# A decoder layer: the score scale moved into the keys, and one output projection by seven products

## The chip, the cores and the metric

The kernel runs on one core of a Trainium2 chip. The metric is the device time of one execution in microseconds; of several runs the median counts. A core has TensorE (PE in the profile), VectorE (DVE), ScalarE (ACT), GpSimd (POOL) and SyncE (SP, which here only issues DMAs). Each engine works its own queue in order, and they wait for each other by semaphores.

## The reference

One layer of a decoder in fp32, with two batch elements of 512 positions and 512 features, layer norm after each residual sum:

```python
x = layernorm(x + attn(x))          # 16 heads of 128, weights = codes * scales (blocks of 32 rows)
x = layernorm(x + xattn(x, memory)) # one head over 1024 memory rows, only the 54 largest scores kept
x = layernorm(x + ffn(x))           # silu(gate) * up, 2048 hidden

# attn
q, k, v = x @ wq + bq, x @ wk + bk, x @ wv + bv
attn = softmax(q @ k.T / sqrt(128)) @ v        # per head
out  = attn @ wo + bo
# xattn
scores = coef * (x @ W_q.T) @ memory.T
att    = softmax(where(scores < 54th largest, -inf, scores))
out    = (att @ memory) @ W_o.T
```

## The kernel before, in words

**Products of blocks.** Nearly all large products are done in blocks of two by two with seven half-size products instead of eight. `seven` issues them: the stationary side and the moving side are each split into four blocks, and sums of blocks are prepared ahead (`combine_a`, `combine_b`, `sums_a`, `sums_b`; four block sums each). Products 1, 6 and 7 accumulate in turn in one PSUM bank `r`, and after each of them ScalarE copies the running sum to `u` (`keep`, line 197, with a bias). So `r` can take the next product only after the copy. Products 2, 5, 4 and 3 go to two or three areas `z`; VectorE adds `z` and `u` in two steps, `on_second` after product 4 and `on_first` after product 3. Product 3 is held back until the next group has begun (`open_product`, `close`). With `late`, product 2 is issued ahead of product 1.

**PSUM.** `r` has two banks, `t` two (single-bank tiles), and `z` two double tiles of two banks. Scores use `z` too: `sc` for the query tiles 0 and 1 takes one, for 2 and 3 the other.

**Attention.** A unit is one head of one element, 32 in all; four units with the same element make a phase, which has one product for the values (`values`) and one for the output (`project`). For each unit `queries_keys` makes q and k (`rqk`, `zqk` in the profile, k added on line 711, q on 712). `weights` makes scores (`sc`, line 748), their negative maximum on VectorE (line 759), multiplies it by 1/sqrt(128) on ScalarE (line 760), takes the exponential with scale 1/sqrt(128) and that bias (line 763, with the row sum), multiplies by the inverse sum (line 772), transposes 32 by 32 blocks on VectorE (line 775) and finishes the transposition with 16 DMAs (line 783). `attend` multiplies with the values two units later (`av`, line 795).

**Second half.** For element 0 the cross-attention runs among the last units of element 1; its search for the 54th largest score (lines 485 to 503) is spread over VectorE's queue. For element 1 the cross queries and scores follow (`seven_xquery`, `seven_xscores`, tiles `xq`, `xs`), and the search and transposition are spread over the feed-forward of element 0: `up` works one 128-wide hidden block after another (`wgu` loaded by SP, block sums `wc` by POOL, `rgu` and `zgu` on TensorE, SiLU on line 1087, gate product on line 1088, `hc` sums of the hidden activations), and `down` multiplies eight hidden blocks back (`rpd`, `zpd`). After `up(0, 1)` and before `down(0, 1)` stands `xattend(1)`: the attention output `xo` by two groups of seven products (`rxav`, `zxav`), then the output product `xpo` (line 597) by plain full-width matmuls, four for each of four position tiles. Layer norm "b" of element 1, its transposition `x2T` and the feed-forward of element 1 follow.

**Order.** The program is written as above, and the framework's scheduler then orders the instructions of each engine; it may place a product of one group between those of another. Semaphores are counted for each engine. Tiles of one tag share a place in memory: a new tile waits until the readers of the old one are done.

```python
    hc = up(0, 1, nc.vector, search1, combine_wdn(0, 1))
    for _ in search1:
        pass
    for _ in xattend(1, ("ot0", "ot1")):
        pass
    layernorm(1, "b")
```

Of the kernel before, what the change touches and what calls it, by code (L numbers as in the profile page):

```python
# [10 lines left out]
F32 = mybir.dt.float32  # L11
AF = mybir.ActivationFunctionType
ALU = mybir.AluOpType
# [11 lines left out]
def decoder_layer(  # L25
# [52 lines left out]
    def place(tag, shape, name):  # L78
        return sb.tile([P, *shape], F32, tag=tag, name=name)
# [85 lines left out]
    def close():  # L165

        if open_product:
            open_product.pop()()

    def seven(name, stat, mov, cols, on_second, on_first, bias=(0.0, 0.0), late=False, piece=None):  # L170


        n = seven_count[0] % 2
        seven_count[0] += 1
        r = bank("r", f"r{name}")[:, :HS]
        if piece:

            zs = [bank("t", f"z{name}_{i}")[:, :HS] for i in range(2)] + [double(f"z{name}", (4, HS))[:, 2, :]]
        else:
            z = double(f"z{name}", (4, HS))  # L180
            zs = [z[:, i, :] for i in range(3)]
        u = place(f"u{n}", (3, HS), f"u{name}")

        def product(i, o, start=True):
            left, right = chunks(stat[i]), chunks(mov[i])
            for k in range(len(left)):
                nc.tensor.matmul(  # L187
                    o,
                    left[k][:, cols],
                    right[k],  # L190
                    start=start and k == 0,
                    stop=k == len(left) - 1,
                    skip_group_check=not start,
                )

        def keep(i, at):
            nc.scalar.activation(u[:, i, :], r, AF.Identity, bias=at)  # L197

        if late:
            product(2, zs[1])  # L200
        product(1, r)
        keep(0, bias[0])
        if not late:
            product(2, zs[1])
        product(5, zs[2])
        product(6, r, False)
        keep(1, bias[0])
        close()
        product(7, r, False)
        keep(2, bias[1])  # L210
        if piece:
            piece(zs[2], u[:, 2, :], 1, 1)
            piece(zs[1], u[:, 0, :], 0, 0)
        product(4, zs[0])
        if piece:
            piece(zs[0], u[:, 2, :], 1, 0)
        else:
            on_second(z[:, 0::2, :], u[:, 2:3, :].to_broadcast([P, 2, HS]))

        def rest():  # L220
            product(3, zs[2], False)
            if piece:
                piece(zs[2], u[:, 1, :], 0, 1)
            else:
                on_first(z[:, 1:3, :], u[:, 0:2, :])

        open_product.append(rest)
# [348 lines left out]
    def xattend(b, ot_tags):  # L576

        oth = [place(tag, (2, S), f"xo{b}_{n}") for n, tag in enumerate(ot_tags)]
        ot = [t[:, n, :] for t in oth for n in range(2)]
        for m in range(HK):  # L580
            seven(
                f"xav{b}_{m}",
                mems[b],
                ats[b],
                slice(m * P, (m + 1) * P),
                lambda z, u, m=m: put(ot[HK + m], z, u, b == 1),
                lambda z, u, m=m: put(ot[m], z, u, b == 1),
            )
            yield
        close()  # L590

        order = [(t, k) for t in range(NT) for k in (0, 2, 3, 1)]
        if b == 0:
            order = [(0, 0), (0, 2), (0, 3), (1, 0), (1, 2), (1, 3), (0, 1), (1, 1)] + order[8:]
        po = [bank("rt"[t % 2], f"xpo{b}_{t}") for t in range(NT)]
        for t, k in order:
            nc.tensor.matmul(
                po[t],
                ot[k][:, t * P : (t + 1) * P],
                xw["wo"][:, k, :],  # L600
                start=(k == 0),
                stop=(k == 1),
                skip_group_check=True,
            )
            if k == 1:
                nc.vector.tensor_add(res[b, t], po[t], res[b, t])
# [93 lines left out]
    def queries_keys(u):  # L700

        g, b, j = units[u]
        h = g * GH + j
        qt = place(f"q{u % 2}", (2, HS), f"q{u}")
        kt = place(f"k{u % 2}", (2, HS), f"k{u}")
        seven(
            f"qk{u}",
            qkw[u],
            xcs[b],
            slice(0, P),  # L710
            lambda z, c: nc.vector.tensor_add(kt, z, c),
            lambda z, c: nc.vector.tensor_add(qt, z, c),
            (bq_sb[:, h : h + 1], bk_sb[:, h : h + 1]),
        )
        qs[u], ks[u] = qt.rearrange("p n s -> p (n s)"), kt.rearrange("p n s -> p (n s)")

    def first_queries_keys():

        z = double("zqk0", (2, S))
        for k in range(KD):  # L720
            for n in range(2):
                nc.tensor.matmul(
                    z[:, n, :],
                    raw["qk0"][0][:, k, n, :],
                    xts[0][:, k, :],
                    start=k == 0,
                    stop=k == KD - 1,
                )
        qs[0] = place("q0", (S,), "q0")
        ks[0] = place("k0", (S,), "k0")  # L730
        nc.scalar.activation(qs[0], z[:, 0, :], AF.Identity, bias=bq_sb[:, 0:1])
        nc.scalar.activation(ks[0], z[:, 1, :], AF.Identity, bias=bk_sb[:, 0:1])

    def weights(u):

# [2 lines left out]
        for t in range(NT):  # L738
            if t % 2 == 0:

                if u == 0 and t:
                    pair = [bank("t", f"sc{u}_{t}_{n}") for n in range(2)]
                else:
                    scs = double(f"sc{u}_{t}")
                    pair = [scs[:, n, :] for n in range(2)]
                nms = small.tile([P, 2], F32, tag="nm", name=f"nm{u}_{t}")
                for n in range(2):
                    nc.tensor.matmul(  # L748
                        pair[n],
                        q[:, (t + n) * P : (t + n + 1) * P],  # L750
                        k,
                        start=True,
                        stop=True,
                    )
                if u == 0 and t:
                    for n in range(2):
                        nc.vector.reduce_max(nms[:, n : n + 1], pair[n], axis=AX.X, negate=True)
                else:
                    nc.vector.reduce_max(nms, scs, axis=AX.X, negate=True)  # L759
                nc.scalar.mul(nms, nms, HSCALE)  # L760
            pr = place(f"p{t}", (S,), f"p{u}_{t}")
            sm = small.tile([P, 1], F32, tag="sm", name=f"sm{u}_{t}")
            nc.scalar.activation(  # L763
                pr,
                pair[t % 2],
                AF.Exp,
                bias=nms[:, t % 2 : t % 2 + 1],
                scale=HSCALE,
                accum_out=sm,
            )  # L770
            nc.vector.reciprocal(sm, sm)  # L771
            nc.scalar.activation(pr, pr, AF.Copy, scale=sm)  # L772


            nc.vector.transpose(  # L775
                tq[:, :, :, t, :].rearrange("p n k c -> p k n c"),
                pr.rearrange("p (k n a) -> p k n a", n=NB, a=BLK),
            )
# [81 lines left out]
    for k in range(KD):  # L860
        nc.scalar.dma_start(out=first[0][k], in_=wqk_first[0][:, k])
        nc.sync.dma_start(out=xts[0][:, k, :], in_=xT[0, k * P : (k + 1) * P, :])
    nc.sync.dma_start(out=bqkv_sb, in_=bqkv)
    for n in range(2):
        nc.scalar.dma_start(out=first[1][n], in_=wqk_first[1][:, n * HK : (n + 1) * HK])
    for h in range(2):
# [171 lines left out]
            nc.gpsimd.tensor_tensor(c[3][:, w], b10[:, w], c[1][:, w], ALU.subtract)  # L1038
            yield

    def up(b, half, eng, search=iter(()), between=iter(())):


        hs, c = [], []
# [20 lines left out]
        for n in range(NH):  # L1065
# [7 lines left out]
            )  # L1073
            if n > 1:
                next(between, None)
            ut = place(f"k{n % 2}", (2, HS), f"ut{i}_{b}")

            def second(z, u, ut=ut):
# [25 lines left out]
    def down(b, half, hc, last_one=False):  # L1104

        for s in range(NT // 2):

            def add(z, u, t):
                o = res[b, t].rearrange("p (c f) -> p c f", c=2)
                if last_one:  # L1110
                    nc.vector.tensor_add(o, o, u)
                    nc.vector.tensor_add(o, z, o)
                else:
                    nc.vector.tensor_add(o, z, o)  # L1114
                    nc.gpsimd.tensor_tensor(o, o, u, ALU.add)  # L1115
# [51 lines left out]
    down(0, 0, hc)  # L1167
    load_wdn(0, 1)
    search1 = chain(search1, turn_weights(1, 2, ("ot0", "ot1"), ("cmb0", "cmb1"), ("v0", "work")))
    hc = up(0, 1, nc.vector, search1, combine_wdn(0, 1))  # L1170
    for _ in search1:
        pass
    for _ in xattend(1, ("ot0", "ot1")):
        pass
    layernorm(1, "b")
    turn_x(1, "v0", "v1", "x2T")
    combine_turned(nc.vector, 1, "v0", "x2")
# [79 lines left out]
```

## Time and profile before

| | |
|---|---|
| median of 3 runs | 1094.98 us (1094.96 to 1095.44) |
| the profiled execution | 1093.37 us |
| its span, first to last instruction | 1091.6 us |
| mean granted TensorE clock | 0.999 |
| PE busy | 1076.9 us (99%) |
| DVE, ACT, POOL busy | 628.3, 411.4, 546.5 us |
| cross-attention output of both elements (`xpo`, line 597) | 64 passes, 28.3 us busy |
| maximum's scaling (line 760) | 64, 12.9 us busy |

A matmul in fp32 is two instructions in the trace, here called passes, each with its weight load (PEld). The mean length of a pass in the profile (381 ns at 256 columns, 592 at 512) is longer than the distance between two of them, since they overlap; the distance is what counts. A number in brackets after a row is the engine's idle time just before it, with what ended it. A line number can be that of a helper: all products of `seven` stand under line 187, all copies of `keep` under 197, and the tile names tell them apart.

### The profile page before, as it was taken

Reading aid. Unit: us, or ns where it says so; the run is one execution under the profiler, and the core shown is the slowest. Engines: PE = TensorE matmul, PEld = TensorE weight load, DVE = VectorE, ACT = ScalarE, POOL = GpSimd, SP = SyncE. Lnnn points to the kernel's source line nnn. Section 1 sums busy time; section 2 is a strip of 40 time slices with the busy share of each in tenths; the row PEclk is TensorE's granted clock in tenths of the full one; section 3 lists DMA queues with packets and bytes.
Section 4 is the critical chain, followed back from the end, with each engine's and each line's share of the span. In section 5 each row is a group of like instructions: output and inputs, shape, how many; then the busy total and the mean of one; then the engine's idle time right before and its main releaser. Section 6 shows DMA issues by size and latency. Waiting matters only on the chain.

```text
span 1091.6 us, 12812 instructions
## 1 busy us (share of the span) xinstructions
PE 1076.9 (99%) x4230; PEld 794.4 (73%) x4230; DVE 628.3 (58%) x1027; ACT 411.4 (38%) x937; POOL 546.5 (50%) x546
## 2 busy tenths in 40 slices
PE   9999999999999999999999999999999999999997
PEld 6676776677677677665666568668888886888886
DVE  5445445346345446643898874568999634543354
ACT  3454435335344433733444453322543211221221
POOL 4965715845844844513852553651565720454620
PEclk9999999999999999999999999999999999999999
DMA  9635546555554365535332535431223411522201
GB/s 349 193 101 156 189 107 209 183 162 153 182 173 125 122 195 146 185 90 178 135 116 80 158 98 205 135 97 39 97 77 119 132 40 25 169 82 73 97 20 39
DMA packets 66256, 142.70 MB, mean 131 GB/s; under 512 B 12560, under 2 KB 12560, under 8 KB 66192
## 3 DMA queue, kind: packets, MB, share of 16 engines
q1 hardware_dynamic: 65328, 139.80, 40.6%
q10 hardware_dynamic: 864, 2.10, 0.5%
q8 instruction: 34, 0.56, 0.2%
q14 instruction: 30, 0.25, 0.1%
HBM read 99.90 MB, written 2.10 MB: 93 GB/s over the span
## 4 chain that ended last, share of the span: by engine, by line
PE 75%; DVE 13%; ACT 4%; DMA 3%; SPq 2%; issue 1%; POOL 1%; ACTq 0%; DVEq 0%; POOLq 0%
PE sc L748 9%; PE av L795 9%; PE zqk L187 8%; PE zgu L187 7%; PE rqk L187 6%; PE zo L187 5%; PE rgu L187 5%; PE zv L187 5%; PE ro L187 4%; PE zpd L187 3%; PE rv L187 3%; DVE work L491 3%; DVE top L494 3%; PE zxav L187 2%; PE rpd L187 2%; PE rxav L187 2%
## 5 line engine op out<-in xcount | busy, mean ns | idle before, releaser
L795 PE MATMUL av<-pt,v 128*128 128x512 f32 x256 | 121.8, 592 | 0.0
L748 PE MATMUL sc<-k,q 128*128 128x512 f32 x256 | 116.8, 597 | 0.0
L759 DVE TENSOR_REDUCE nm<-sc 128x2 f32<-128x1024 f32 x63 | 76.8, 1223 | 66.8 <-PE sc L748 66.8
L107 POOL TENSOR_TENSOR wc<-wqk 128x256 f32<-128x256 f32 x31 | 24.2, 782 | 162.6 <-PE zqk L187 161.6
L775 DVE STREAM_TRANSPOSE tq<-p 128x512 f32<-128x512 f32 x128 | 85.0, 699 | 35.1 <-ACT p L772 28.7
L748 PEld LDWEIGHTS sc<-k,q 128*128 128x128 f32 x256 | 47.6, 190 | 58.0 <-issue 50.9
L648 POOL TENSOR_TENSOR wqk<-wqk,sqk 128x512 f32<-128x512 f32 x52 | 65.0, 1269 | 46.9 <-DMA wqk<-in_wqk 33.6
L763 ACT ACTIVATE p<-sc,nm 128x512 f32<-128x512 f32 x128 | 86.8, 685 | 1.5
L772 ACT ACTIVATE p<-p,sm 128x512 f32<-128x512 f32 x128 | 86.2, 722 | 0.6 <-DVE sm L771 0.6
L197 ACT ACTIVATE ugu<-rgu 128x256 f32<-128x256 f32 x96 | 36.0, 378 | 99.2 <-PE rgu L187 97.1
L795 PEld LDWEIGHTS av<-pt,v 128*128 128x128 f32 x256 | 48.6, 190 | 30.5 <-issue 26.8
L197 ACT ACTIVATE uqk<-rqk,bqkv_sb 128x256 f32<-128x256 f32 x93 | 43.9, 472 | 64.4 <-PE rqk L187 64.4
L187 PE MATMUL rgu<-x2c,wc 128*128 128x256 f32 x256 | 66.1, 381 | 1.0 <-ACT ugu L197 1.0
L187 PE MATMUL rqk<-x0c,wc 128*128 128x256 f32 x248 | 64.8, 384 | 0.3
L187 PEld LDWEIGHTS rqk<-x0c,wc 128*128 128x128 f32 x248 | 45.5, 190 | 19.4 <-ACT uqk L197 9.9
L107 POOL TENSOR_TENSOR wc<-wgu 128x256 f32<-128x256 f32 x32 | 25.4, 794 | 67.9 <-DMA wgu<-in_wgu 35.1
L494 DVE MAX8 top<-work 128x8 f32<-128x1024 f32 x48 | 58.7, 1223 | 0.9
L1115 POOL TENSOR_TENSOR res<-res,upd 128x512 f32<-128x512 f32 x12 | 15.8, 1313 | 78.3 <-DVE res L1114 73.7
L187 PEld LDWEIGHTS rgu<-x2c,wc 128*128 128x128 f32 x256 | 48.2, 190 | 8.8 <-ACT ugu L197 1.7
L813 ACT ACTIVATE ot<-av,bqkv_sb 128x512 f32<-128x512 f32 x28 | 19.2, 686 | 81.1 <-PE av L795 81.1
L491 DVE MATCH_REPLACE8 work<-top,work 128x1024 f32<-128x1024 f32 x40 | 48.4, 1210 | 0.0
L648 POOL TENSOR_TENSOR wv<-wv,sv 128x512 f32<-128x512 f32 x24 | 29.9, 1269 | 31.1 <-DMA wv<-in_wv 31.1
(285 smaller groups left out, 2432.0 us busy)
## 6 DMA issues: line engine op xcount, KB each, us to landing
pt<-tq SPq DMA_DIRECT2D x512, 64.0 KB, 2.0
wgu<-in_wgu SPq DMA_DIRECT2D x32, 512.0 KB, 3.2
wqk<-in_wqk SPq DMA_DIRECT2D x26, 512.0 KB, 3.9
sqk<-in_wqk_s SPq DMA_DIRECT2D x26, 512.0 KB, 4.0
wdn<-in_wdn SPq DMA_DIRECT2D x8, 1024.0 KB, 5.8
sv<-in_wv_s SPq DMA_DIRECT2D x14, 512.0 KB, 5.7
wv<-in_wv SPq DMA_DIRECT2D x7, 1024.0 KB, 5.6
wo<-in_wo SPq DMA_DIRECT2D x7, 1024.0 KB, 5.6
```

The lines of the kernel that those rows point to most:

```text
L107: eng.tensor_tensor(c[0], a10, a11, ALU.add)
L187: nc.tensor.matmul(o, left[k][:, cols], right[k], start=start and k == 0, stop=k == len(left) - 1, skip_group_check=not start,)
L197: nc.scalar.activation(u[:, i, :], r, AF.Identity, bias=at)
L491: nc.vector.match_replace(work, top, src, LOWEST)
L494: nc.vector.max(top, work)
L648: eng.tensor_tensor(part[:, w], codes[:, w], sct[:, w], ALU.mult)
L748: nc.tensor.matmul(pair[n], q[:, (t + n) * P : (t + n + 1) * P], k, start=True, stop=True,)
L759: nc.vector.reduce_max(nms, scs, axis=AX.X, negate=True)
L763: nc.scalar.activation(pr, pair[t % 2], AF.Exp, bias=nms[:, t % 2 : t % 2 + 1], scale=HSCALE, accum_out=sm,)
L772: nc.scalar.activation(pr, pr, AF.Copy, scale=sm)
L775: nc.vector.transpose(tq[:, :, :, t, :].rearrange("p n k c -> p k n c"), pr.rearrange("p (k n a) -> p k n a", n=NB, a=BLK),)
L795: nc.tensor.matmul(av, vs[u // GH][:, k, j * P : (j + 1) * P], pt[:, :, k, :], start=(k == 0), stop=(k == NT - 1),)
```

## The change

**Scale.** The factor 1/sqrt(128) goes into the keys. `seven` gets a `scale` for its third copy, k is made with `scalar_tensor_tensor` (z times the factor plus u), the key's bias is scaled once into `bks`, and the scaling of the maximum and the scale of the exponential go.

**Output of the second element by seven products.** For element 1 `xattend` makes block sums of `xo` as its chunks come (VectorE, `first`), and multiplies with the output weights by two groups `xpo` of `seven`. The weights' sums `woc` are made by POOL in the place "v1". This whole cross-attention is moved ahead of the last hidden block of `up(0, 1)` (`other`); `up`'s search is emptied first.

**With it.** `late` issues product 4 early too, right behind product 2 (cross scores of element 1 and the new product). `down` of the second half (`if half`) adds `u` and `z` both on VectorE, where before POOL added `u` (element 0).

```diff
     def seven(..., late=False, piece=None, scale=1.0):
...
         if late:
             product(2, zs[1])
+            product(4, zs[0])
         product(1, r)
...
-        keep(2, bias[1])
+        keep(2, bias[1], scale)
...
-        product(4, zs[0])
+        if not late:
+            product(4, zs[0])
...
+        o4, sums = [t[:, :, h] for h in (slice(0, HS), slice(HS, S)) for t in oth], []
+        if b == 1:
+            c12 = [place(f"p{n}", (HK, HS), f"xoc{n}") for n in range(2)]
+            c4 = place("wqk0", (HK, HS), "xoc_4")
+
+        def first(z, u, m):
+            put(ot[m], z, u, b == 1)
+            if b == 1:
+                c = [f[:, m : m + 1] for f in (*c12, c4)]
+                sums.append(sums_a(nc.vector, o4, [[f] for f in c], [slice(m, m + 1)]))
+                next(sums[-1])
+                for left in sums if m else ():
+                    next(left)
...
         close()
+        if b == 1:
+            stat = ALEFT(o4, (*c12, o4[2], c4))
+            for s in range(NT // 2):
+
+                def add(z, u, t):
+                    o = res[b, t].rearrange("p (c f) -> p c f", c=2)
+                    nc.vector.tensor_add(o, o, u)
+                    nc.vector.tensor_add(o, z, o)
+
+                seven(
+                    f"xpo{b}_{s}",
+                    stat,
+                    xw["woc"],
+                    slice(s * P, (s + 1) * P),
+                    lambda z, u, s=s: add(z, u, 2 + s),
+                    lambda z, u, s=s: add(z, u, s),
+                    late=s == 0,
+                )
+            close()
+            return
...
-            lambda z, c: nc.vector.tensor_add(kt, z, c),
+            lambda z, c: nc.vector.scalar_tensor_tensor(kt, z, HSCALE, c, ALU.mult, ALU.add),
             lambda z, c: nc.vector.tensor_add(qt, z, c),
-            (bq_sb[:, h : h + 1], bk_sb[:, h : h + 1]),
+            (bq_sb[:, h : h + 1], bks[:, h : h + 1]),
+            scale=HSCALE,
...
-                nc.scalar.mul(nms, nms, HSCALE)
...
                 bias=nms[:, t % 2 : t % 2 + 1],
-                scale=HSCALE,
...
+    bks = const.tile([P, H], F32, name="bks")
+    nc.scalar.mul(bks, bk_sb, HSCALE)
...
+            if other and n == NH - 1:
+                for _ in search:
+                    pass
+                for _ in other:
+                    if sums:
+                        sums.pop()()
...
-                if last_one:
+                if half:
                     nc.vector.tensor_add(o, o, u)
                     nc.vector.tensor_add(o, z, o)
...
-    hc = up(0, 1, nc.vector, search1, combine_wdn(0, 1))
-    for _ in search1:
-        pass
-    for _ in xattend(1, ("ot0", "ot1")):
-        pass
+    def attended_early():
+        xw["woc"] = combine_b(nc.gpsimd, blocks(xw["wo"]), place("v1", (4, HK, HD), "woc"))
+        yield from xattend(1, ("ot0", "ot1"))
+
+    hc = up(0, 1, nc.vector, search1, combine_wdn(0, 1), attended_early())
```

The changed order that the scheduler makes of it is known too, without times: ScalarE takes three of a unit's four exponentials before the multiplications by the inverse sums and the fourth after three of these; TensorE's next `rqk` begins after the scores instead of before them; and the products of the last hidden block stand behind those of the new output product.

More of the change, by code (lines that the diff above doesn't have):

```diff
@@ L168, in close, with seven @@
             open_product.pop()()
-    def seven(name, stat, mov, cols, on_second, on_first, bias=(0.0, 0.0), late=False, piece=None):
+    def seven(name, stat, mov, cols, on_second, on_first, bias=(0.0, 0.0), late=False, piece=None, scale=1.0):
         n = seven_count[0] % 2
@@ L194, in product, with keep @@
                 )
-        def keep(i, at):
-            nc.scalar.activation(u[:, i, :], r, AF.Identity, bias=at)
+        def keep(i, at, scale=1.0):
+            nc.scalar.activation(u[:, i, :], r, AF.Identity, bias=at, scale=scale)
         if late:
             product(2, zs[1])
+            product(4, zs[0])
         product(1, r)
@@ L586, in xattend @@
                 lambda z, u, m=m: put(ot[HK + m], z, u, b == 1),
-                lambda z, u, m=m: put(ot[m], z, u, b == 1),
+                lambda z, u, m=m: first(z, u, m),
             )
@@ L731, in first_queries_keys @@
         nc.scalar.activation(qs[0], z[:, 0, :], AF.Identity, bias=bq_sb[:, 0:1])
-        nc.scalar.activation(ks[0], z[:, 1, :], AF.Identity, bias=bk_sb[:, 0:1])
+        nc.scalar.activation(ks[0], z[:, 1, :], AF.Identity, bias=bks[:, 0:1], scale=HSCALE)
     def weights(u):
@@ L1039, in combine_wdn, with up @@
             yield
-    def up(b, half, eng, search=iter(()), between=iter(())):
+    def up(b, half, eng, search=iter(()), between=iter(()), other=None):
         hs, c = [], []
```

## The prediction

> **What bounds the kernel now.** I read the page first, then the groups kept apart by form, then TensorE's timeline, and last the chain of waits inside one attention unit.
>
> ```profile
> PE 1076.9 (99%) x4230; PEld 794.4 (73%) x4230; DVE 628.3 (58%) x1027; ACT 411.4 (38%) x937; POOL 546.5 (50%) x546
> PEclk9999999999999999999999999999999999999999
> ```
>
> TensorE is busy all through and at full clock; no other engine passes 58%. A busy PE need not be at its peak, so the next question is what a matmul costs at its best.
>
> ```profile
> 902.08 12.18 PE L597 MATMUL xpo<-wo,xo 128*128 128x512 f32 x28
> 914.10 1.89 PE L187 MATMUL rpd<-wdn,h 128*128 128x256 f32 x8
> 915.82 1.89 PE L187 MATMUL zpd<-wdn,h 128*128 128x256 f32 x8
> ```
>
> Each matmul stands in the trace as two passes. Eight half-width passes take 1.72 us from start to start (914.10 to 915.82), so 0.216 us each and 0.43 us a matmul. Twenty-eight full-width passes take 902.08 to 914.10: 0.429 each, 0.86 a matmul. The program has 1,755 half-width, 344 full-width and 32 narrow matmuls: 758 + 296 + 7 = 1061 us. The span of 1091.6 is only 31 above that, of which about 10 lie before the first weights and after the last matmul. So a change can win by fewer matmul columns, or out of some 20 us of small stalls. Where those lie, one unit shows (timeline, other engines' rows left out):
>
> ```profile
> 284.04 1.22 DVE L759 TENSOR_REDUCE nm<-sc 128x2 f32<-128x1024 f32 x1 [3.60 <-PE sc L748]
> 285.30 0.20 ACT L760 ACTIVATE nm<-nm 128x2 f32<-128x2 f32 x1 [2.29 <-DVE nm L759]
> 285.54 0.69 ACT L763 ACTIVATE p<-sc,nm 128x512 f32<-128x512 f32 x1
> ...
> 287.23 1.33 ACT L772 ACTIVATE p<-p,sm 128x512 f32<-128x512 f32 x2
> ...
> 288.46 0.20 ACT L760 ACTIVATE nm<-nm 128x2 f32<-128x2 f32 x1
> 288.69 0.69 ACT L763 ACTIVATE p<-sc,nm 128x512 f32<-128x512 f32 x1
> ...
> 290.73 1.02 PE L795 MATMUL av<-pt,v 128*128 128x512 f32 x2
> ...
> 291.26 0.46 ACT L197 ACTIVATE uqk<-rqk,bqkv_sb 128x256 f32<-128x256 f32 x1
> 291.77 1.13 PE L187 MATMUL rqk<-x0c,wc 128*128 128x256 f32 x4
> ```
>
> PE is free at 291.59 (290.73 + 0.86) and waits to 291.77 for ScalarE's copy `uqk`: 0.18, and 0.10 more because the next pass also starts late. ScalarE is late because it works this queue in order. Four units (77.5 us, 262.9 to 340.4) hold seven such places: `rqk` behind `uqk` 0.28 twice, `sc` behind q 0.20 twice, the z bank behind the exponentials 0.28 twice, `zo` 0.19. Together 1.7 us a phase.
>
> **Part 1: no scaling instruction.** It removes the 64 scalings of L760 on ScalarE (0.20 us each), two in each unit and both on the path above. The first put the exponential at 285.54 instead of 285.30. Walked again in the changed order with these durations: exponentials at 285.30, 285.97; `uqk` 286.64; third exponential 287.02 (its maximum ends at 286.98); then three multiplies 0.61 apart to 289.52; fourth exponential 289.52; the second `uqk` at 290.18, done 290.65 instead of 291.72. The changed PE order uses that: the `av` that stood before `rqk` now stands behind it, and `rqk` wants to start at 290.73. The stall goes, with only 0.03 to spare. What is late next: q. From the last `zqk` to `sc` there are again two 0.86 pieces, and `sc` still loses 0.20. For the z bank the second exponential ends 0.24 earlier, which covers the 0.18 fully in the units before a value product and half of it before a projection. A phase keeps about 0.2 + 0.2 + 0.2 + 0.2 = 0.8 and gains 1.0. Units 4 to 22 are 4.5 phases: -4.5. Units 0 to 3, where the same waits are mixed with loads: -1.5.
>
> Against it: where the order differs from the regular one, copies stand behind the multiplies. At unit 23 `rqk` and `rv` wait 0.22 and 0.72 for `uqk`, with two refills 1.1. In units 28 to 31, where DVE also runs the top-54 search, unit 31 and its projection wait 0.17 + 0.29 + 0.40 + 0.10 and four refills, less 0.3 that go: +1.0. I take +2.1; below it could be 0, above it 4 (each search pair of 1.2 + 1.2 us that slips ahead of a k or q costs up to 2.4).
>
> The key's tensor_add becomes scalar_tensor_tensor. No row shows that form at 512 with a PSUM input. L500, twice as long, takes 1.27 at its shortest and half is 0.64; the replaced add took 0.68. I take 0.68. Longer costs nothing up to 0.3: `rqk` ends 291.8, `uqk` 292.3, k 293.0, and the product that waits for k starts at 293.3. A gain has no place, since q follows later. The new `bks` waits for the biases ahead of nothing urgent: the two weight DMAs stay before it in ScalarE's queue, `alpha` ran at 10.71 and k at 13.82. Zero, at most 0.3. SP's queue has some weight loads moved past 16 `pt` DMAs (10 us); they land a unit or more ahead of their use. Zero, and the same for POOL's dequantising that moved with them.
>
> **Part 2: seven products for the output.** Sixteen full-width matmuls (13.7 us: 902.08 to 914.10 and one earlier at 898.64) become 28 half-width (28 x 0.43 = 12.1): -1.65. One rule speaks against it. The Trainium skill, "TensorE: Matmul & The Clock Gate", Back-to-back issue gap, gives for streams of weight load and matmul 81 ns at 128 columns and 131 at 512. Its line gives 98 at 256, three quarters of a full-width one, and 28 x 0.75 = 21 would cost a third more than 16: +4.2 here. This trace has the half at 0.216 against 0.429 all through, weight loads hidden; I use the trace.
>
> The added work: four POOL sums for `woc` (1.27 each). Three stand ahead of the weights' sums for hidden block 13, the fourth among them. POOL did those at 853.2 for use at 858.9; 3.8 us later the first is done at 857.7, and the third sum 859.2 against 859.7. Free, by half a microsecond. Eight DVE sums of 256 (0.42) and two more adds lie under 24 us of `zxav` products. The last hidden block now follows the attention, so its SiLU stands behind four normalisations (2.9 us) and one of two new table loads (1.28). Counted from the last `zxpo` product: statistics and normalisations to +6.9, load to +8.4, SiLU +9.0, h +9.7; PE needs h at +10.6 after gu15 and ten products of `down`. Free by 0.8. The skill's "ScalarE: Activation LUTs", What ACT_TABLE_LOAD costs, gives a drain of 1.38 after each load, which would turn 0.8 spare into a stall of 0.6. Here the load at 837.39 took 1.28 and the next ACTIVATE began at 838.69, so I see no drain; 0.6 goes into the range.
>
> **Part 3: smaller moves.** With `late`, product 4 comes early in the cross scores and fills 0.86 where PE waited 0.56 for DVE's `qt` at 728.16 (0.8 with refill): -0.8, at least 0. `down` adds both halves on DVE: 0.69 more work each, while the x2T sums that blocked `zpd` at 939.01 (0.58) come six microseconds earlier: -0.45, between -0.7 and +0.5.
>
> **Sum.** -4.5 - 1.5 + 2.1 - 1.65 - 0.8 - 0.45 = -6.8. With 0.03 to spare at every second unit I give back eight refills: -6.0. The profiled execution itself took 1093.37 us, span 1091.6; the median of the runs is 1.6 higher, 1094.98. I take the difference over: 1089.0.
>
> **Rivals.** (a) As summed: 1086.8 to 1091.2. (b) The next rung is as late as the last: ScalarE's queue is only reordered, PE takes the same stalls at other places, and parts 2 and 3 alone count against +2.1 late: -0.8, 1094. For it: 0.03 spare. Against it: two instructions really leave the path. (c) Half of that, with the search stage at its upper end: 1092. (d) Slower, by the key: scalar_tensor_tensor with a PSUM input takes as long as L500 does for twice the elements, 1.27. The 0.3 spare is exceeded by 0.3, with refill 0.4 in each of 31 units, +12, in sum 1101. It decides from 1.0 us a key upward. Against it: L500 runs at the rate of a plain add. (e) The change does not do what it says: a scheduler moves the products so that h is late at `down`; no more than 1.5 us, inside (a) and (c).
>
> **How the numbers follow.** (a) 0.74, (c) 0.10, (b) 0.11, (d) 0.05. About 0.2% (2.2 us) is what a measurement of this kernel can tell from no change, so faster means below 1092.8: (a) and most of (c), 0.83; within 0.2%, 0.12; slower 0.05. The range leaves out (d), most of (b) and the ends: 1086.2 to 1092.8.
>
> **What would show it.** L760 gone; `uqk` no longer named as the wait of `rqk` in regular units; `sc` behind q still there; `k` at 0.7; `zxpo` at 0.216 a pass; no PE gap before `zpd` of the second half. Wrong if the gaps of `rqk` and z remain, if k is over 1 us, or if PE idles at `down`.

## The result, and the profile after

The changed kernel takes 1096.59 us (median of 22 runs, 1094.35 to 1098.79); the kernel before, beside it, 1094.69 (22 runs, 1093.65 to 1095.44). The ratio is 1.0018, 95% interval 1.0013 to 1.0024: about 1.9 us slower. Predicted were 1089.0. The profiled execution took 1098.04 us with a span of 1096.3, so it is 1.5 above its median, while the profiled execution before (1093.37) was 1.3 below. The two traces therefore differ by more (4.7 us) than the medians do.

The page of the changed kernel has TensorE still busy all through, 24 passes more and less busy time:

```profile
PE 1073.9 (98%) x4254; PEld 801.0 (73%) x4254; DVE 641.5 (59%) x1043; ACT 408.6 (37%) x882; POOL 546.2 (50%) x546
```

What was lost must lie between the passes. For all that follows I call *stall* the distance between the starts of two consecutive TensorE passes, less 0.216 us after a pass of 256 columns and 0.429 after one of 512 (the distances that the prediction read off the trace). The 32 narrow products stand as one pass each, 0.109 from start to start; that is 3.5 us and not the 7 of the prediction's bound, and nothing rests on it. The second pass behind a wait also starts 0.10 late; I call that the *refill*. Summed over the trace it is 27.6 us before and 34.0 after: +6.4. Twenty-eight half-width products for sixteen full-width ones take 1.65 less. Together +4.7, the difference of the spans.

First the rows that went as predicted. The groups of the changed kernel (busy us, then mean ns of one) show k by `scalar_tensor_tensor` at the price of an add, 688 ns:

```profile
L747 DVE SCALAR_TENSOR_TENSOR k<-zqk,uqk 128x512 f32<-128x512 f32 x31 | 21.3, 688 | 10.4 <-ACT uqk L197 7.4 <-PE zqk L187 3.0
```

Its timeline shows the new output product at 0.216 a pass (907.45 to 908.32 is four passes):

```profile
907.45 1.03 PE L187 MATMUL zxpo<-woc,xoc 128*128 128x256 f32 x4
908.32 1.03 PE L187 MATMUL rxpo<-woc,xoc 128*128 128x256 f32 x4
```

And the regular unit (the same head as the one shown before; timeline of the changed kernel, rows of other instructions left out):

```profile
285.51 0.69 ACT L799 ACTIVATE p<-sc,nm 128x512 f32<-128x512 f32 x1 [2.29 <-DVE nm L796]
...
287.95 1.94 ACT L807 ACTIVATE p<-p,sm 128x512 f32<-128x512 f32 x3
...
289.78 0.68 ACT L799 ACTIVATE p<-sc,nm 128x512 f32<-128x512 f32 x1
...
290.45 0.47 ACT L197 ACTIVATE uqk<-rqk,bqkv_sb 128x256 f32<-128x256 f32 x1
...
290.97 1.13 PE L187 MATMUL rqk<-x0c,wc 128*128 128x256 f32 x4
```

No scaling instruction is left, and the second `uqk` starts at 290.45. TensorE is free at 290.08 + 0.86 = 290.94 and starts `rqk` at 290.97: the wait of 0.18 is 0.03, though the refill of 0.10 behind it stays (1.13 for four passes in place of 1.03). So far the walk was right.

Now the unit that contains a projection (`ro`, `zo`), one in four. Timeline before, then after; q is the last operand that the scores wait for, `otc` a sum of the attention output:

```profile
256.49 0.69 DVE L117 TENSOR_TENSOR otc<-ot,otc 128x512 f32<-128x512 f32 x1 [1.24 <-ACT ot L813]
...
257.10 0.68 DVE L712 TENSOR_TENSOR q<-zqk,uqk 128x512 f32<-128x512 f32 x1
...
257.84 3.70 PE L748 MATMUL sc<-k,q 128*128 128x512 f32 x8
...
259.86 1.23 DVE L759 TENSOR_REDUCE nm<-sc 128x2 f32<-128x1024 f32 x1 [0.35 <-PE sc L748]
...
262.86 1.13 PE L187 MATMUL zqk<-x0T,wqk 128*128 128x256 f32 x4
```

```profile
255.18 0.69 DVE L748 TENSOR_TENSOR q<-zqk,uqk 128x512 f32<-128x512 f32 x1 [1.38 <-PE zqk L187]
...
255.93 3.70 PE L785 MATMUL sc<-k,q 128*128 128x512 f32 x8
...
256.76 1.17 DVE L117 TENSOR_TENSOR otc<-ot,otc 128x512 f32<-128x512 f32 x1 [0.89 <-ACT ot L848]
...
257.46 1.05 POOL L110 TENSOR_TENSOR wc<-wqk,wc 128x256 f32<-128x256 f32 x1
...
257.85 1.21 DVE L118 TENSOR_TENSOR otc<-ot,ot 128x512 f32<-128x512 f32 x1
...
258.98 1.21 DVE L796 TENSOR_REDUCE nm<-sc 128x2 f32<-128x1024 f32 x1
...
261.73 1.13 PE L187 MATMUL zqk<-x0T,wqk 128*128 128x256 f32 x4 [0.80 <-ACT p L799]
```

Before, one of these sums stood ahead of q and two behind it, and VectorE had been idle for 0.35 us when the scores let the maximum begin, 2.02 us after the first score product. After, the maximum starts 3.05 us after it, with no idle time ahead of it: VectorE was still making sums. TensorE's new order has the scores 1.9 us earlier (255.93 against 257.84), while the sums begin no earlier than before, so the two between q and the maximum now hold it up, and they take 1.17 and 1.21 in place of 0.69 while GpSimd runs its `wc` sums (e1 takes this up). The maximum is an us late, so are the exponentials, and `zqk` starts 0.97 us late, with 0.10 refill behind it. Before, this stall was 0.18 and 0.10.

### The profile page after: what moved, and what is told of

Same layout as the page of the kernel before. It is cut to its first block, busy times and chain, and to the rows that moved or that the text cites. A ratio compares the mean times of both kernels' runs of the same rounds, so it can differ in the third digit from the quotient of the medians.

```text
span 1096.3 us, 12758 instructions
## 1 busy us (share of the span) xinstructions
PE 1073.9 (98%) x4254; PEld 801.0 (73%) x4254; DVE 641.5 (59%) x1043; ACT 408.6 (37%) x882; POOL 546.2 (50%) x546
## 4 chain that ended last, share of the span: by engine, by line
PE 75%; DVE 16%; ACT 4%; DMA 2%; issue 1%; POOL 1%; SPq 1%; DVEq 0%; ACTq 0%; POOLq 0%
PE av L830 9%; PE zqk L187 9%; PE sc L785 8%; PE zgu L187 7%; PE rqk L187 6%; PE rgu L187 5%; PE zo L187 5%; PE zv L187 4%; DVE work L493 4%; DVE top L496 3%; PE ro L187 3%; PE rv L187 3%; PE zpd L187 3%; PE rpd L187 3%; PE zxav L187 2%; PE rxav L187 1%
## 5 line engine op out<-in xcount | busy, mean ns | idle before, releaser
L1128 DVE TENSOR_TENSOR gt<-zgu,ugu 128x512 f32<-128x512 f32 x32 | 21.9, 684 | 45.0 <-PE zgu L187 44.9
L748 DVE TENSOR_TENSOR q<-zqk,uqk 128x512 f32<-128x512 f32 x31 | 21.3, 688 | 38.1 <-PE zqk L187 38.1
```

## The experiments

All were run beside the kernel before, whose median was 1094.66 to 1094.77 in each set. Stalls from the profile of each kernel, by stretch of the kernel before (us of its span; in the other kernels the same share of the work):

| stretch | before | changed | changed again (e4) | scale only (e1) | output only (e2) | before + sums on POOL (e5) | changed + sums on POOL (e3) | e3 again (e11) |
|---|---|---|---|---|---|---|---|---|
| 0–63 | 4.99 | 4.44 | 4.50 | 4.51 | 4.90 | 4.94 | 4.50 | 4.50 |
| 63–127 | 1.51 | 1.84 | 1.83 | 1.84 | 1.52 | 1.49 | 0.86 | 0.86 |
| 127–360 (three phases) | 5.16 | 5.85 | 5.86 | 5.59 | 5.21 | 5.30 | 3.02 | 3.03 |
| 360–437 | 1.64 | 2.41 | 2.13 | 2.60 | 1.65 | 1.50 | 1.40 | 1.01 |
| 437–637 (with the search) | 4.36 | 6.38 | 5.31 | 6.38 | 4.36 | 4.06 | 4.05 | 5.07 |
| 637–end | 9.93 | 13.06 | 11.82 | 10.62 | 11.64 | 11.70 | 9.07 | 9.23 |
| sum | 27.6 | 34.0 | 31.5 | 31.5 | 29.3 | 29.0 | 22.9 | 23.7 |

The stretches before 360 repeat to a few hundredths from one profile to the next where the order is the same, but for e1's 5.59 (below). Those behind do not: e3 and e11 are one kernel and differ by 0.4 and 1.0 there.

**e1, the scale alone.** Of the change only `bks`, the `scale` of `seven`, k's `scalar_tensor_tensor` and the removed scalings.

> The kernel before with only the scale of the scores put into the keys; the cross attention's output stays at sixteen full-width products. Theory A, now held: taking the two scaling instructions away reorders the queues, and the gain at rqk and at the value products is smaller than what is lost where a 1.2 us instruction of VectorE now stands ahead of a maximum or of q: about +4 us, 1097 to 1099 (ratio 1.003 to 1.004). The stall of zqk behind the exponentials is 0.9 us in every fourth unit, against 0.28 before. Rival B, the prediction's sum of part 1: -4.5 - 1.5 + 2.1, so 1090 to 1092 (ratio 0.997).

1097.26 us, ratio 1.0025 (1.0014 to 1.0036). Slower, as theory A says; rival B, the prediction's own sum, is out. Up to 736 us TensorE and ScalarE have the changed kernel's order, and the first five stretches hold the same stall in sum (20.9): the loss belongs to this part.

The profiles also tell how this loss is made. In the unit shown above the first of the two sums took 0.69 in e1 and the second 1.22, and the stall of `zqk` is 0.49 in place of 0.97. At all twenty such places (five each in changed, e4, e1 and e10) the stall, without refill, is what the two sums took over 0.69 each, to within 0.04: 0.9 for sums of 1.1 and 1.2, 1.76 for 1.37 and 1.75, 1.98 for 1.59 and 1.75. So the new order takes away the slack, and the longer sums make the stall; with both sums at 0.69 next to nothing of it would be left, by an estimate from these places.

**e2, the output alone.** The change without the scale (ScalarE multiplies the maximum again).

> The kernel before with only the second element's cross-attention output by seven products, the hidden block moved behind it, product 4 early in the first cross scores and the two adds of the second half on VectorE; the scores are scaled on ScalarE as before. Theory A: parts 2 and 3 give what was summed for them, -1.65 - 0.8 - 0.45 = -2.9, with some 0.5 lost again: 1092 (ratio 0.9975). Rival C: the stalls that part 3 takes away come back at the next wait, and only fewer matmul columns count: -1.65, 1093 (ratio 0.9985).

1092.80 us, ratio 0.9982 (0.9974 to 0.9990): -1.9 us. That lies between A (-2.9) and C (-1.65). Its attention is the old one to 0.1 us. Behind 637 its profile has 1.7 us more stall than before, so this profile shows none of the gain (both spans are 1091.6); only the medians do. In this profile TensorE waits 0.54 and 1.80 us for the sums `x1c` of the cross query, against 0.73 before; e9 and e10 look at that wait.

**e3, the sums on GpSimd.** One word in the changed kernel:

```diff
         oc = combine_b(
-            nc.vector,
+            nc.gpsimd,
             (lo[:, :, :HS], lo[:, :, HS:], hi[:, :, :HS], hi[:, :, HS:]),
```

> The changed kernel with the sums of the attention output (otc, L116 to L119 of project) on GpSimd in place of VectorE. In the regular units TensorE and ScalarE keep the changed kernel's order. Theory A: the maximum no longer stands behind a 1.2 us sum, zqk after ro no longer waits 0.9 us (at most 0.1) at five places and 1.5 at a sixth, so -4 to -5 against the changed kernel: 1092. Rival D: those stalls come from the exponentials' own chain (maximum, two exponentials), not from the sums: the stall stays above 0.6 and the time within 1 us of 1096.6. Rival E: the sums come late from GpSimd, and ro or zo wait for otc: slower than 1097.

1087.78 us, ratio 0.9942 (0.9929 to 0.9954): 8.8 below the changed kernel and 6.9 below before. The same unit in its timeline:

```profile
254.11 3.70 PE L785 MATMUL sc<-k,q 128*128 128x512 f32 x8
...
256.14 1.22 DVE L796 TENSOR_REDUCE nm<-sc 128x2 f32<-128x1024 f32 x1 [2.08 <-PE sc L785]
256.33 1.26 POOL L117 TENSOR_TENSOR otc<-ot,otc 128x512 f32<-128x512 f32 x1
...
258.95 1.08 PE L187 MATMUL zqk<-x0T,wqk 128*128 128x256 f32 x4
```

The maximum starts 2.03 us after the first score, and `zqk` waits for nothing to speak of. Up to 590 us TensorE and ScalarE keep the changed kernel's order, so only the place of the sums differs there. A phase of four units has 1.0 us of stall in place of 1.95. Against the profile of e4, which lies nearer to the changed kernel's median than the first one, the stalls fall by 8.6, of which 4.5 lie before 437, as A put it. D and E are out (once, at 419 us, `ro` does wait 0.55 for a sum of GpSimd). The search stage and the end gave 4.0 more, which A did not have; the order of the search changed there too, and no run separates what did it.

**e4, the changed kernel once more.**

> The changed kernel a second time, for one more look. If the 3.4 us at half of TensorE's clock behind the wait for x1c (723 us) come by chance, the granted clock is 1.0 through that stage here and the span is about 1.7 us shorter, near 1094.6. If they belong to the kernel, 0.5 shows again. The stalls of zqk after ro (0.9 us) and of the last sc (1.2) should be there again.

1095.54 us, span 1093.8, 2.5 less than the first profile. The stalls of the attention up to 360 are the same to 0.06. The stall of `zqk` is there again. The clock stayed at 1.0 behind the wait for x1c, so the half clock does not come in every execution (below). The last `sc` waits 0.36 in place of 1.18.

**e5, the sums on GpSimd in the kernel before.** The edit of e3 made in before.

> The kernel before with one edit: the sums of the attention output (otc) on GpSimd; scores scaled on ScalarE as before, plain output product as before. It asks what the scale in the keys is worth by itself once no sum stands ahead of a maximum. Theory A: the waits of rqk (0.28) and of the value products (0.28) stay, because ScalarE still holds the two scaling instructions; 1.5 to 1.7 us of stalls a phase of four units against 1.0 in the third experiment (the changed kernel with these sums on GpSimd); 1092 to 1094. Rival F: all the gain of the third experiment came from relieving VectorE, and the scale is worth nothing: 1.0 a phase here too, and 1089 to 1090 (what remains are the seven products).

1094.60 us, ratio 1.0002 (0.9993 to 1.0010). Moving the sums is worth nothing without the scale: 1.77 us a phase, with the old waits of 0.28. With the scale, 1.0. Rival F is out. (Two passes of `ro` a phase moved with it in TensorE's queue. Its profile also has the half clock, and the median is a little above what A gave.) So neither edit gains alone, scale +2.6 and sums -0.1, and together, with the output's part in it, -5.6 to -6.9. Scale and sums without the output were not run; less the 1.9 of e2 they would be at about -4 to -5, an estimate.

**e6, the adds of the second half back on GpSimd**, in e3 (`if half:` to `if last_one:`).

> The third experiment (changed kernel, otc on GpSimd, 1087.8) with the second half's residual add o+u of the first element back on GpSimd, as before the change. The prediction put the move of these adds to VectorE at -0.45. If that holds: 1088.2, with a wait of zpd at the second half near 0.7 us as before. Theory A expects little: the wait there depends on whether an add of two SBUF operands meets a GpSimd sum; in the third experiment it did not (0.22 us). Within 0.5 us of 1087.8 either way.

1092.19 us, ratio 0.9976 (0.9965 to 0.9986): 3.0 to 4.4 above the two runs of e3, where under 0.5 was expected by both views. The wait of `zpd` is small here (0.42). What is late is another: the layer norm of element 0 waits for GpSimd's add, its square root stands ahead of `ugu` in ScalarE's queue, and TensorE waits for that:

```profile
938.35 1.26 POOL L1158 TENSOR_TENSOR res<-res,upd 128x512 f32<-128x512 f32 x1 [2.73 <-DVE res L1157]
...
940.59 0.29 ACT L1189 ACTIVATE sdc<-mvc,eps 128x1 f32<-128x1 f32 x1 [3.70 <-DVE mvc L1187]
940.79 0.36 ACT L197 ACTIVATE ugu<-rgu 128x256 f32<-128x256 f32 x1
...
941.21 1.13 PE L187 MATMUL rgu<-x2c,wc 128*128 128x256 f32 x4 [2.01 <-ACT ugu L197]
```

In e3 this `rgu` follows without a gap. So in the order of e3 the adds are worth 3 us or more on VectorE, by a wait that the prediction had not listed. That is not the gain over the kernel before: there the same add stood on GpSimd too, in another order, and the trace shows no wait of TensorE for `ugu` at this place.

**e7, the plain output product**, in e3: sixteen full-width matmuls, without `woc` and the `xoc` sums, still ahead of the last hidden block.

> The third experiment with the second element's output product as sixteen full-width matmuls in place of twenty-eight half-width ones (no woc sums, no sums of the attended values), still ahead of the last hidden block. By the prediction's term the seven products are worth 1.65 us: 1089.4, span 1086.8. If the rule of a three-quarter price for a half-width matmul decided, it would be 4 us faster than 1087.8. The waits around it (0.3 at zxpo) go with it, so +1.3 to +1.7.

1091.41 us, ratio 0.9970 (0.9958 to 0.9982): 2.2 to 3.6 above e3. The sign excludes a three-quarter price (the prediction's estimate between the two figures of its rule), which would have made it 4 us faster. The size is not clean: its profile has a stall of 2.0 at a `zpd` of element 0's second half (0.22 with refill in e3), where an add and a sum of VectorE met GpSimd's `dc` sums (they took 1.58 and 1.75 us).

**e9 and e10, GpSimd held until x1c is summed.** In all of the kernels above, TensorE waits at x1c of the second element's cross query, where `dc` sums of the down weights start on GpSimd at about the same time. A semaphore wait makes them start behind x1c; every engine keeps its order. e9 is e3 with it, e10 the changed kernel with it.

```diff
+        def behind_x1(one):
+            if b + half == 0:
+                tc.add_manual_dep(
+                    one.ins,
+                    x1_done[0].ins.name,
...
+                )
+
         for w in steps:
-            nc.gpsimd.tensor_tensor(c[0][:, w], b01[:, w], b00[:, w], ALU.subtract)
+            behind_x1(nc.gpsimd.tensor_tensor(c[0][:, w], b01[:, w], b00[:, w], ALU.subtract))
...
```

> The third experiment (changed kernel, otc on GpSimd) with one wait more: GpSimd's sums of the down weights (dc, the first half) start only when VectorE's four sums x1c of the cross query are done. Every engine keeps its order. If it is the meeting with GpSimd that stretches x1c's sums (1.75 and 1.15 us in place of 0.68), they run at 0.7 here, the wait of rxq falls from 0.89 to under 0.2 and that of zxq behind it from 0.65 to under 0.4; -1 to -1.4 us in span, 1086.5 to 1087, and no half clock there. If the sums are slow for another reason (the operands' layout), the waits stay, and the time is 1087.8 or a little more.

> The changed kernel with the same one wait for GpSimd's dc sums. In its executions x1c's sums took 1.75, 1.74 and 1.15 us, rxq waited 1.96, and in one of two profiles TensorE's clock was halved for 3.4 us behind it. If the meeting with GpSimd is the cause: the wait falls under 0.2, the clock stays at 1.0, and the median falls by 2 to 3 us, to 1094; the spread of the runs (4.4 us) narrows.

e9 1088.47 us (0.9944, 0.9931 to 0.9956), e10 1095.21 (1.0006, 0.9998 to 1.0014). The cause of the wait is shown, the gain is not. Timeline of the changed kernel, then of e9, at the same sums (the helper's line is 189 in e9):

```profile
719.65 3.00 POOL L1068 TENSOR_TENSOR dc<-wdn 128x512 f32<-128x512 f32 x2 [4.67 <-DMA wdn<-in_wdn]
719.77 1.75 DVE L118 TENSOR_TENSOR x1c<-x1T 128x512 f32<-128x512 f32 x1
...
721.45 1.74 DVE L117 TENSOR_TENSOR x1c<-x1T,x1c 128x512 f32<-128x512 f32 x1
...
723.34 1.10 PE L187 MATMUL rxq<-x1c,wqc 128*128 128x256 f32 x4 [1.79 <-DVE x1c L117]
```

```profile
712.50 0.68 DVE L117 TENSOR_TENSOR x1c<-x1T,x1c 128x512 f32<-128x512 f32 x1
...
713.51 1.03 PE L189 MATMUL rxq<-x1c,wqc 128*128 128x256 f32 x4
...
722.12 1.27 DVE L144 TENSOR_TENSOR qc<-qt 128x256 f32<-128x256 f32 x1
...
723.42 1.37 DVE L145 TENSOR_TENSOR qc<-qc,qt 128x256 f32<-128x256 f32 x1
...
725.51 1.13 PE L189 MATMUL zxq<-x1T,wqc 128*128 128x256 f32 x4 [1.63 <-DVE qt L399]
```

With GpSimd held, the same sums take 0.67 to 0.69 in both kernels, TensorE does not wait for them, and the clock stays at 1.0 there. But the held sums now run against the next ones, `qc`, which take 1.27 and 1.37, and `zxq` waits 1.63 (in e10 too) where e3 waited 0.55. The stall was moved by ten us. Both expectations of the size missed: e9 stands between the two runs of e3, and e10 is only 1.4 below the changed kernel.

**e8, a longer wait** (e3 with the sums x1c computed twice over), to see what the wait itself does to the clock.

> The third experiment with the four sums x1c of the second element's cross query computed twice over, so that TensorE waits longer there. It asks whether a wait of a few us by itself brings the half clock that one of three executions with a 1.8 us wait showed. If a pause of about 3 us halves TensorE's clock: granted clock 0.5 for some 3 us behind the wait, and about 1.7 us more than the longer wait itself. If not: clock 1.0 behind it, and the span longer by the wait alone (2 to 4 us over 1085.2).

1096.51 us (one run), span 1094.7. TensorE stood 5.3 us; the clock fell to 0.5 in the course of this wait, 2.3 us after TensorE had gone idle, and stayed there until 3.9 us behind it. The span is 9.5 longer than in e3, more than either case of the expectation gave; 6.2 of it lie at this wait and its half clock, the rest elsewhere. The last section takes the clock up.

**e11, e3 once more.**

> The third experiment a second time, as the yardstick beside the two others of this call and to see which of its stalls come by chance: within 1 us of 1087.8; the attention part's stalls as in the first profile (1.0 us a phase), those behind it within 2 us of the 9.1 found there.

1089.21 us, ratio 0.9948 (0.9934 to 0.9961), 0.4 outside the expected 1 us; the attention up to 360 repeats to 0.01, while the two stretches behind it differ by 0.4 and 1.0 in the same order. The stalls behind 637 are 9.2, within what was expected. The changed kernel with these sums on GpSimd is the fastest kernel here, 5.6 to 6.9 us below before in two sets of runs.

## Why the prediction was wrong

**Part 1, the regular units: mechanism right, place of the next wait wrong.** `rqk` fell from 0.28 to 0.11 as walked, with the 0.03 to spare just missed; the stall of the value product went; `sc` behind q stayed at 0.19 and `zo` at 0.19. The step that failed is "for the z bank the second exponential ends 0.24 earlier, which covers ... half of it before a projection". I put the remainder at about 0.2; it is 1.0 to 1.1 (0.91 to 0.97 and refill) at four places, and more at a fifth near 418 us. The walk moved ScalarE's and TensorE's instructions into their new order, but took the maximum's end from the old trace, of a unit without a projection. In the new order q and the scores come ahead of the next `rqk` and the first `ro`, which stood before them (255.93 against 257.84, of which 0.4 had been gained earlier). The slack of 0.35 us that the attention output's sums had ahead of the maximum is gone, and each of the two left there takes 0.5 longer beside GpSimd. A phase lost 0.2 where it was to gain 1.0. That the sums make this stall is shown by e3, where it is gone; that it is as long as their lengthening is shown by the twenty places counted at e1.

**Its size without that.** With the sums off VectorE a phase has 1.0 us of stall; against e5, where they are off too, the scale brings 0.77 a phase (1.77 to 1.0), against 1.0 predicted. The first stretch (units 0 to 3) gained 0.5 and not 1.5. The attention in all, to 637 us, went from 17.7 to 20.9 (e4: 19.6) against -3.9 predicted; in e3 it is 13.8. That is the 3.9 less that was predicted, and e3's medians (1087.8 and 1089.2) lie at the 1089.0, but this is luck: the prediction was for the sums on VectorE, and even in e3 a phase gained 0.7 and not 1.0, while the stretch from 437 to 637, put at +2.1, moved by -0.3 and +0.7.

**Part 1, the late places: right.** The copies behind the multiplies at unit 23 cost 0.38 at `rqk` and 0.90 at `rv` against 0.33 before, +0.95 where +1.1 was put. The warning that a search step may slip ahead of a q came true at the last unit (changed kernel):

```profile
640.19 2.20 DVE L502 SCALAR_TENSOR_TENSOR s<-s,top,work 128x1024 f32<-128x1024 f32 x1 [1.13 <-ACT work L500]
...
642.33 0.68 DVE L748 TENSOR_TENSOR q<-zqk,uqk 128x512 f32<-128x512 f32 x1
...
643.06 3.70 PE L785 MATMUL sc<-k,q 128*128 128x512 f32 x8 [1.01 <-DVE q L748]
```

Before, q stood ahead of that step. The step itself took 2.20 in place of 1.28, with GpSimd running; in e4, in the same place of the queue, it took 1.39 and `sc` waited 0.36. From 437 us to the last `zo`, less the 0.95 of unit 23, the stalls grew by 0.8 (e4) to 2.6 (first profile), against +1.0.

**The key's form: right.** 0.69, no cost; rival (d) is out.

**Part 2: right.** The half-width passes cost 0.216, `woc` came in time, h was not waited for at `down`, and no drain showed: the table load at 916.99 took 1.28, and the square root behind it began at 918.28. Three refills at the new product give back 0.3 of the 1.65. By the medians of e2 parts 2 and 3 are worth 1.9, between the 1.65 and their sum of 2.9.

**Part 3: one step wrong, one right in sign.** Product 4 of the cross scores does not fill the wait of `zxq` for `qt`: on TensorE it stands behind it. The wait goes with the length of the two sums `qc` that VectorE makes ahead of `qt`: they take 0.43 each in the changed kernel's first profile and in e2, and there it is only the refill; 0.72 to 0.88 in before, e3 and e4, and it is 0.55 to 0.70; 1.27 and 1.37 in e9 and e10, and it is 1.63. The first profile and e4 are one kernel, and e5, without the early product 4, has only the refill as well: product 4 gave nothing here. The adds of `down`: the stall at `zpd` of element 0 (939 us before) grew from 0.74 to 1.19 in the changed kernel, and that at the `down` after it (992) fell from 0.98 to 0.43, -0.1 against -0.45; but taking them back in the order of e3 cost 3 us or more (e6).

**The rivals.** Rival (b), "the next rung is as late as the last", named the outcome's kind and was given 0.11; its 1094 took the new waits to be as long as the old. They were longer, since the new order leaves two sums of VectorE that meet GpSimd no slack in front of the maximum. Rival (d) had VectorE in it, but only by the key's form; none had VectorE's queue. That was the gap: the changed order of VectorE was at hand, and its sums were not priced behind q.

## What to carry to other kernels

When an edit changes the order of the queues, walk every engine's new order with its instructions' durations, not only the engine that the edit relieves: an instruction that had slack in the old order can be the last to end in the new one. Take its duration from where the other engine works beside it, not from where it runs alone. An edit that gains nothing alone (the sums on GpSimd) can be what another needs to gain; test the two together. A wait that comes from two engines meeting is not removed by moving one of them: look at what it meets next.

## What the runs showed of the hardware

**VectorE and GpSimd in each other's way.** From the trace of the changed kernel I counted VectorE's sums and products of 512 elements. With both operands in SBUF and GpSimd idle they take 0.68 us (43 of them, 0.67 to 0.69). With GpSimd working over half of their time: median 1.17, up to 1.75 (31 of them, of which seven took no more than 0.69). e9 and e10 show that GpSimd is the cause: with it held, the same sums fall from 1.75 to 0.68. With one operand in PSUM they take 0.69 either way (132 beside GpSimd, none over 0.69), and so do the 32 by 32 transposes (0.71) and the maximum (1.23). The groups show it in the means, 680 for the sum that runs early, mostly alone, and 1136 for one that does not:

```profile
L118 DVE TENSOR_TENSOR otc<-ot,ot 128x512 f32<-128x512 f32 x7 | 8.0, 1136 | 0.0
...
L116 DVE TENSOR_TENSOR otc<-ot 128x512 f32<-128x512 f32 x7 | 4.8, 680 | 0.0
```

The Trainium skill, "GPSIMD Engine Reference", Specifications, says that GpSimd's SBUF interfaces are shared with VectorE and that instructions with two SBUF inputs contend. That agrees for most of them; the size, 1.7 times at the median and up to 2.6, is from here. A stall of this kind can differ between two executions of one kernel: the search step above took 2.20 and 1.39. GpSimd's sums often start when a DMA lands (the row at 719.65 above waited 4.67 for one), which would explain it; no run isolated that.

**Pauses of 1.8 and 0.5 us and a half clock of TensorE.** The windows view (busy time of PE, PEld, DVE, ACT and POOL with count, then the granted clock, DMA share and GB/s) of the changed kernel, around the wait for x1c:

```profile
721.00:725.00 4.00, 1.73 (x8) 0.90 (x6) 3.96 (x5) 0.01 (x1) 4.00 (x3) 1.00 0.00 0
725.00:728.40 3.40, 3.40 (x8) 2.69 (x9) 2.16 (x5) 2.92 (x6) 3.40 (x3) 0.50 0.00 0
728.40:735.00 6.60, 6.60 (x32) 5.80 (x31) 3.93 (x10) 1.88 (x5) 5.29 (x7) 1.00 0.29 69
```

For 3.4 us a pass takes twice as long, which costs 1.7 us. The waits ahead of it were 1.79 and 0.48 us with some work between. Of four profiles with these waits (changed, e2, e4, e5), two show it (changed and e5); of six with waits of 0.73 and 0.48 there (before, e1, e3, e6, e7, e11), none; of two with one of 1.63 (e9, e10), none; e8, with 5.3 us, does. The half clock lasts 3.41 us in changed and in e5, and 6.83, twice that, in e8. The Trainium skill, "TensorE: Matmul & The Clock Gate", Why this matters for your kernels, warns of idle gaps of more than about 3 us; here less was enough in two of four profiles; what decides between them no run shows. It fits the wider spread of the changed kernel's runs (4.4 us, against 1.8), though no run isolated that; e10, without the wait, still spread over 3.5 us.
